# Column tiles of 64 for every matmul but the transposes, with a new order of the period's steps, in a two-layer graph network kernel

## The chip, the cores and the metric

The kernel runs on one core of one Trainium2 chip. The metric is the device time of one execution in microseconds (us). PE is the matrix engine, DVE the vector engine, ACT the scalar engine, POOL the GpSimd engine and SP the engine whose queue issues most DMAs. PSUM is the memory that PE writes, in banks of 2 KB in each of 128 partitions; SBUF is the working memory.

## The reference

There are B = 128 graphs of N = 128 nodes with F = 64 features, in fp32. Layer 0 is an edge network over the nonzero entries of `adj`, layer 1 a three-layer network over aggregated features. Both are residual with a layer norm.

```python
# layer 0: mask of edges, an edge function relu(a_j + c_k) summed over k
mask = (adj > 0)
diff = x[:, :, None, :] - x[:, None, :, :]
h  = relu((x @ W1a)[:, :, None, :] + diff @ W1b + b1)       # H = 192
hm = einsum('bjkh,bjk->bjh', h, mask)
x  = layernorm(x + hm @ W2 + deg[..., None] * b2)
# layer 1
agg = einsum('bmn,bnd->bmd', adj, x)
h = elu(agg @ V1 + c1); h = elu(h @ V2 + c2)                  # 128 wide
out = layernorm(x + h @ V3 + c3)
```

## The kernel before

Two graphs are taken together as one pair p, so that 2 x 64 features fill 128 partitions; there are 64 pairs. Everything in layer 0 is sparse. Nodes are sorted by their degree (`prepare`: the mask `mk`, degrees `deg`, `keys`, ranks, a permutation `permb`), and nine blocks of sorted nodes (`BLOCKS`: first node, last node, slots) give each node as many slots as its degree may need. In `sort_mask` nine instructions `oh` on DVE write, for each block, a one-hot matrix of the neighbour that sits in each slot, by comparing `vp` with `slotc`, both in SBUF, in bf16. For each pair and block there is a unit of three steps: ACT copies `aj` into a PSUM bank `e` (L914), PE adds the gathered `cp[k]` of the neighbours, as 18 matmuls of 64 output partitions (L924), and DVE sums absolute values over the slots (`sums`, L934). `cp` holds the projected features in three bf16 parts that add up to fp32; `project_c` makes it (C, L712 and L715, two banks, then `r` L726 on DVE, `cp` L722 and L729 on ACT and L731 on POOL). `sort_x` sorts the features and projects them to `aj` (L610, L617), and then makes a correction for unused slots: `sa` on POOL (L624), the `short` product, `ea` on DVE (L639) and `corr` on POOL (L646). `turn` transposes `adj` and `x`. `finish` is the rest of the pair: `hm` on POOL (L846), projections (L851, L855), un-sorting (L868), `y` and its statistics `st` on DVE (L741, L746), the factors `ve`, `rs`, `nb` on POOL (L753 to L758; `rs` is a power on 128x2 elements), the normed `x` on ACT (L775), then aggregation (L875), `hid1` (L884), `hid2` (L890) and `last` (L895, L897) with ELU steps `r` and `e` on ACT and `h` on DVE between them, and a second norm that ends in the stored output.

All queues are written out by a planner at build time, the class `Flow`. A thread is a generator of steps; a step names its engines, a planned cost, the events that it follows, and how many of the four shared PSUM banks it takes. Each step has a due time in `DUE`, in us from the start of its pair's period, to which `ROUND` = 11.1651 is added for each pair; a negative time is a step made ahead for a later pair. From the first gather until 14 units before the end the planner takes, among the steps that could be planned, the one with the earliest due time. So in each period the order of an engine's queue is that of the due times modulo 11.1651. A list in `DUE` has one time for each step that a thread yields, in order: the last nine of `sort_mask` are the `oh` of units 0 to 8, the last four of `sort_x` are `sa`, `short`, `ea` and `corr`, the first two of `prepare` are `mk` and `keys`, and the last of `project_c` is its step on POOL; a unit has three, for copy, gather and sum. Before and after that stretch it takes the step that is ready first by its planned clocks. The chip executes each engine's queue in order, and waits only for data and for buffers to come free; the planned times do not hold anything back. Two things in the planner stand for the chip: `PORT` is a resource that POOL's steps and the `oh` steps take in turn, and `CHANGE` is a price for PE going from one tiling of its array to another. The modes are "" (full width of 128 columns), "t" (column tiles, 128 rows by 64 columns), "r" (row tiles, 64 by 128), "x" (transposes), and "*", which is column tiles if the step before it was in them and full width otherwise. `stationary` writes a "*" product in the form that the mode asks for:

```python
if flow.mode == "t":
    for h in (slice(0, P // 2), slice(P // 2, P)):
        nc.tensor.matmul(out[h], lhsT(h), rhs, **kw)
else:
    nc.tensor.matmul(out, lhsT(slice(0, P)), rhs, **kw)
```

The edge banks `e` are four, used in turn by the units, so a unit's copy follows the sum of the unit four before it. The last pair's norms are done partly on DVE (`LATE`). After the sparse part, a dense path exists for pairs whose degrees exceed the slots; it is passed over when a count on the chip says that there are none.

Of the kernel before, what the change touches and what calls it, by code (L numbers as in the profile page):

```python
# [87 lines left out]
class Flow:  # L88
# [61 lines left out]
    def _kind(self, mode):  # L150
        return mode if mode != "*" else "t" if self.mode == "t" else ""
# [35 lines left out]
def sparse(tc, env):  # L187
# [18 lines left out]
        "prepare": (-43.06, -42.93, -39.21, -39.08, -35.87),  # L206
        "sort_x": (-26.76, -10.46, -10.33, -3.14, -3.02, 2.5, 2.63, 2.76, 2.89),
        "sort_mask": (-26.12, -25.99, -25.86, -23.42, -23.29, -23.16, -13.67, -13.28, -13.03,
                      -12.77, -2.63, -2.25, -1.99, -1.73),
        "turn": (-36.9, -36.77),  # L210
        "project_c": (-32.15, -29.32, -29.2, -29.07, -28.94, -4.17, -4.04),
        "finish": (12.64, 19.44, 19.57, 21.62, 21.75, 21.88, 22.01, 28.04, 28.17, 29.2, 33.56,
                   33.69, 33.82, 34.71, 43.31, 43.44, 44.47, 44.6, 46.52, 46.65, 48.06, 48.19,
                   59.87),
        "unit": [(-1.48, 0.96, 1.09), (2.12, 2.25, 2.37), (3.02, 3.14, 3.27), (3.66, 3.79, 3.91),
                 (4.68, 4.81, 4.94), (5.07, 5.2, 5.33), (5.97, 6.1, 6.22), (6.35, 6.48, 6.61),
                 (7.25, 11.61, 11.74)],
    }

    DUE["consts_late"] = (  # L220
        12.0, 17.0, 18.5, 19.5, 19.65, 19.66, 19.67, 19.68, 23.0, 24.0, 25.0, 26.0, 27.0, 28.0,
        29.0, 30.0, 31.0, 32.0, 33.0, 34.0, 35.0, 36.0)
# [23 lines left out]
    def stationary(out, lhsT, rhs, **kw):  # L246

        if flow.mode == "t":
            for h in (slice(0, P // 2), slice(P // 2, P)):
                nc.tensor.matmul(out[h], lhsT(h), rhs, **kw)  # L250
        else:
            nc.tensor.matmul(out, lhsT(slice(0, P)), rhs, **kw)  # L252
# [287 lines left out]
    def prepare(p):  # L540
# [19 lines left out]
        def spread(key):  # L560
            for s in range(2):
                stationary(key[:, s * N:(s + 1) * N],
                           lambda h: degb[:, s:s + 1].to_broadcast([P, h.stop - h.start]),
                           identb, start=True, stop=True)
            stationary(key[:, 2 * N:3 * N], lambda h: small[:, h], iotb, start=True, stop=True)
        ev, key = yield ("PE:*", 0.17, [ev] + made("identb", "small", "iotb"), 1, spread)
# [37 lines left out]
    def project_a(p, xsT, ev):  # L604
# [3 lines left out]
        def project(aps):  # L608
            for c in range(3):
                nc.tensor.matmul(aps[:, c * N:(c + 1) * N], wad[:, c, :], xsT,  # L610
                                 start=True, stop=True)
        ev, aps = yield ("PE", 0.66, [ev] + made("wad"), 1, project)
# [36 lines left out]
    def sort_mask(p, ev):  # L649
# [3 lines left out]
        def sort(t):  # L653
            for s in range(2):
                stationary(t[:, s * N:(s + 1) * N], lambda h: d["mk"][:, s, h], permb[:, s, :],
                           start=True, stop=True)
            for s in range(2):
                stationary(t[:, (2 + s) * N:(3 + s) * N], lambda h: permb[:, s, h], identb,
                           start=True, stop=True)
        ev, t = yield ("PE:*", 0.22, [ev], 1, sort)  # L660
# [7 lines left out]
        ev, vps = yield ("PE:*", 0.12, [evm] + made("prefix"), 1,  # L668
                         lambda vps: stationary(vps[:, :2 * N], lambda h: prefix[:, h], flat(mtp),
                                                start=True, stop=True))  # L670
# [33 lines left out]
    def project_c(p, ev):  # L704

        d = S[p]
        cols = H + O

        def project(*cps):
            for s in range(2):  # L710
                k = slice(s * F, (s + 1) * F)
                nc.tensor.matmul(cps[s][:, :cols], d["turned"][k, 2, :], wc[k, :],  # L712
                                 start=True, stop=False)
            for s in range(2):
                nc.tensor.matmul(cps[s][:, H:cols], onesb[:, :P], b2p, start=False, stop=True)  # L715
        ev, *cps = yield ("PE:r", 0.7, [ev] + made("wc", "b2p", "onesb"), 2, project)
        cp = d["cp"] = prep.tile([P, 3, 2, cols], BF16, name="cp", bufs=7)
        r1 = prep.tile([P, 2, cols], F32, name="r1", bufs=4)
        hi = []
        for s in range(2):  # L720
            e, = yield ("ACT", act(cols), [ev], 0,
                        lambda: nc.scalar.copy(cp[:, 0, s, :], cps[s][:, :cols]))  # L722
            hi.append(e)
        for s in range(2):
            ev, = yield ("DVE", dve(cols), [hi[s]], 0,
                         lambda: nc.vector.tensor_sub(r1[:, s, :], cps[s][:, :cols],  # L726
                                                      cp[:, 0, s, :]))
            flow.give(cps[s], ev)
        ev, = yield ("ACT", act(2 * cols), [ev], 0, lambda: nc.scalar.copy(cp[:, 1], r1))  # L729
        ev, = yield ("POOL PORT", 1.12, [ev], 0,  # L730
                     lambda: nc.gpsimd.tensor_sub(cp[:, 2], r1, cp[:, 1]))  # L731
        happened(ev, "cp", p)
# [106 lines left out]
    def finish(p):  # L839
# [8 lines left out]
        def project(yb):  # L848
            cp, mtp = d["cp"], d["mtp"]
            for c in range(3):  # L850
                nc.tensor.matmul(yb[:, :2 * O], hm[:, c, :], flat(w2d[:, c]),  # L851
                                 start=(c == 0), stop=False)
            for s in range(2):
                for i in range(3):
                    nc.tensor.matmul(yb[:, s * O:(s + 1) * O], mtp[:, s, :], cp[:, i, s, H:H + O],  # L855
                                     start=False, stop=(s == 1 and i == 2))
        ev, yb = yield ("PE", 0.85, [ev] + made("w2d"), 1, project)
# [8 lines left out]
        def unsort(t):  # L866
            for s in range(2):
                nc.tensor.matmul(t[:, s * O:(s + 1) * O], d["permT"][:, s, :],  # L868
                                 ys[:, s * O:(s + 1) * O], start=True, stop=True)
        ev, t = yield ("PE", 0.4, [ev, event("permT", p)], 1, unsort)  # L870
# [11 lines left out]
        def hidden1(zb):  # L882
            for s in range(2):
                nc.tensor.matmul(zb[:, s * N:(s + 1) * N], v1p[:, s, :], agg,  # L884
                                 start=True, stop=True)
        ev, zb = yield ("PE", 0.49, [ev] + made("v1p"), 1, hidden1)
        h1, ev = yield from elu(zb, ev, "h1", 0)

        def hidden2(zb):
            nc.tensor.matmul(zb[:, :2 * N], v2s, h1, start=True, stop=True)  # L890
        ev, zb = yield ("PE", 0.48, [ev], 1, hidden2)
        h2, ev = yield from elu(zb, ev, "h2", 1)

        def last(t):
            nc.tensor.matmul(t[:, :2 * O], onesb[:, :P], c3p, start=True, stop=False)  # L895
            for s in range(2):
                nc.tensor.matmul(t[:, s * O:(s + 1) * O], h2[:, s * N:(s + 1) * N], v3s,  # L897
                                 start=False, stop=(s == 1))
        ev, t = yield ("PE", 0.51, [ev] + made("rowp", "v3s"), 1, last)
# [283 lines left out]
```

## Time and profile before

| | |
|---|---|
| median of 3 runs | 752.73 us (752.58 to 753.43) |
| the profiled execution | 754.12 us |
| its span, first to last instruction | 752.3 us |
| mean granted PE clock | 0.992 |
| period in the steady part | 11.18 us, 64 pairs |
| first `sums` of the first pair's last block | 33.1 us after the start |
| HBM traffic | 23 GB/s over the span |

The profile is of one execution. Its page gives the busy time of each engine (PEld is the loading of weights, beside PE), and the chain of work that ended last. Views of the trace give the busy time of each engine in a stretch (the columns are start and end, length, then PE, PEld, DVE, ACT and POOL, each with its number of instructions, the granted clock, the DMA share and GB/s), and a timeline of instructions in order of time: start, length, engine, line, operation, tiles, shape, number. A length is that of the record, and in the timeline instructions that follow each other in one group are one line; the recorded time of an instruction reaches past the start of the next one, because engines are pipelined. What an instruction costs its engine is therefore read from start to start. On PE, 128*64 is a product over 128 rows into 64 columns of the array; an fp32 product appears as two instructions.

### The profile page before, as it was taken

What the parts mean: (1) busy time and instruction counts of PE and PEld (TensorE: products, weight loads), DVE (VectorE), ACT (ScalarE), POOL (GpSimd) and SP (SyncE); (2) the same over time, 40 slices, a digit from 0 to 9 for tenths busy, and PEclk for the clock granted to TensorE, in tenths of its full rate; (3) what the DMA queues carried; (4) which work ended last, traced back from release to release, by engine and by line L of the source; (5) the groups of instructions that cost most, each with busy time, mean ns of one, the idle gap of its engine ahead of it and who ended that gap; (6) DMA issues with size and microseconds to landing.
All of it is one profiled execution on the core that took longest, in us unless ns stands there. A gap on an engine that the chain in (4) does not pass through costs nothing.

```text
span 752.3 us, 36121 instructions
## 1 busy us (share of the span) xinstructions
PE 732.1 (97%) x14791; PEld 667.8 (89%) x14792; DVE 724.3 (96%) x2381; ACT 706.3 (94%) x1986; POOL 432.1 (57%) x801
## 2 busy tenths in 40 slices
PE   7899999999999999999999999999999999999994
PEld 4788999999999999999999999999999999999993
DVE  7999999999999999999999999999999999999984
ACT  4778999999999999999999999999999999999984
POOL 5336557556556556656655655655755655655662
PEclk9999999999999999999999999999999999999997
DMA  4000011011101101101101101101101110110000
GB/s 124 15 3 3 21 27 31 23 26 31 26 21 31 30 18 31 30 19 31 31 17 31 32 16 33 31 21 27 31 24 25 31 26 22 31 27 10 10 14 19
DMA packets 54667, 19.72 MB, mean 26 GB/s; under 512 B 37600, under 2 KB 54496, under 8 KB 54496
## 3 DMA queue, kind: packets, MB, share of 16 engines
q1 hardware_dynamic: 53792, 17.05, 9.3%
q8 instruction: 118, 1.93, 1.1%
q14 instruction: 53, 0.43, 0.2%
q10 hardware_dynamic: 704, 0.30, 0.1%
HBM read 13.14 MB, written 4.19 MB: 23 GB/s over the span
## 4 chain that ended last, share of the span: by engine, by line
PE 93%; DVE 3%; ACT 2%; issue 1%; DMA 0%; POOL 0%; ACTq 0%; POOLq 0%; DVEq 0%
PE e L924 45%; PE m L610 6%; PE m L851 5%; PE m L712 5%; PE m L890 4%; PE m L884 4%; PE m L897 4%; PE m L868 3%; PE m L694 3%; PE m L250 3%; PE m L596 2%; PE m L875 2%; PE m L855 1%; PE m L715 1%; PE m L252 1%; PE m L695 1%
## 5 line engine op out<-in xcount | busy, mean ns | idle before, releaser
L924 PE MATMUL e<-oh,cp 128*64 128x162 bf16 (+3 forms) x10368 | 385.5, 228 | 3.5 <-ACT e L914 3.3
L924 PEld LDWEIGHTS <-cp 128*64 128x64 bf16 x10368 | 350.2, 110 | 16.6 <-issue 4.9
L934 DVE TENSOR_REDUCE sums<-e 128x54 f32<-128x486 f32 (+8 forms) x576 | 335.1, 611 | 6.8 <-PE e L924 2.0
L914 ACT COPY e<-aj 128x504 f32<-128x504 f32 (+6 forms) x576 | 293.6, 542 | 8.0 <-DVE sums L934 7.4
L753 POOL TENSOR_SCALAR ve<-st 128x2 f32<-128x2 f32 x126 | 24.1, 191 | 242.4 <-DVE st L746 232.0
L679 DVE TENSOR_TENSOR oh<-vp,slotc 128x308 bf16<-128x308 bf16 (+6 forms) x576 | 150.3, 321 | 1.0 <-ACT vp L672 0.2
L754 POOL TENSOR_TENSOR rs<-ve,mhalf 128x2 f32<-128x2 f32 x126 | 87.8, 697 | 10.5
L731 POOL TENSOR_TENSOR cp<-r,cp 128x512 bf16<-128x512 f32 x64 | 74.3, 1160 | 29.8 <-ACT cp L729 29.8
L646 POOL TENSOR_TENSOR corr<-ea,sa 128x384 f32<-128x384 f32 x64 | 64.2, 1003 | 9.9 <-DVE ea L639 4.9
L624 POOL TENSOR_TENSOR sa<-aj,srow 128x384 f32<-128x384 f32 x64 | 64.6, 1009 | 2.9 <-ACT aj L617 2.9
L795 ACT ACTIVATE r<-m,cc 128x256 f32<-128x256 f32 x128 | 61.4, 480 | 5.1 <-PE m L884 3.1
L846 POOL TENSOR_TENSOR hm<-sums,corr 128x384 f32<-128x384 f32 x63 | 63.3, 1004 | 5.1 <-DVE sums L934 5.1
L617 ACT ACTIVATE aj<-m,b1c 128x128 f32<-128x128 f32 x192 | 56.6, 365 | 8.2 <-PE m L610 1.8
L801 DVE SCALAR_TENSOR_TENSOR h<-m,cc,e 128x256 f32<-128x256 f32 x128 | 60.6, 473 | 2.0 <-ACT e L798 1.9
L798 ACT ACTIVATE e<-r 128x256 f32<-128x256 f32 x128 | 54.4, 426 | 2.1
L610 PE MATMUL m<-xsT,wad 128*128 128x128 f32 x384 | 54.4, 278 | 0.0
L851 PE MATMUL m<-w2d,hm 128*128 128x128 f32 x384 | 53.7, 276 | 0.0
L775 ACT ACTIVATE x<-y,nb,rs 128x64 f32<-128x64 f32 x126 | 49.1, 442 | 0.2 <-POOL nb L757 0.2
L610 PEld LDWEIGHTS m<-xsT,wad 128*128 128x128 f32 x384 | 48.5, 194 | 0.3
L726 DVE TENSOR_TENSOR r<-m,cp 128x256 f32<-128x256 f32 x128 | 47.9, 416 | 0.5 <-ACT cp L722 0.5
L851 PEld LDWEIGHTS m<-w2d,hm 128*128 128x128 f32 x384 | 48.0, 192 | 0.4 <-POOL hm L846 0.4
L712 PE MATMUL m<-wc,turned 64*128 64x256 f32 x256 | 46.4, 436 | 1.7 <-DVE r L726 1.7
(157 smaller groups left out, 1333.1 us busy)
## 6 DMA issues: line engine op xcount, KB each, us to landing
adj<-in_adj_dram SPq DMA_DIRECT2D x64, 128.0 KB, 2.7
xx<-in_x_dram SPq DMA_DIRECT2D x64, 64.0 KB, 2.7
out_dram<-o SPq DMA_DIRECT2D x64, 64.0 KB, 1.6
w1s<-in_L_gnn_W_dram ACTq DMA_DIRECT2D x2, 96.0 KB, 3.0
w2s<-in_L_gnn_W_dram ACTq DMA_DIRECT2D x2, 48.0 KB, 2.6
v2s<-in_L_gnn_W_dram SPq DMA_DIRECT2D x1, 64.0 KB, 2.2
v1d<-in_L_gnn_W_dram SPq DMA_DIRECT2D x2, 32.0 KB, 2.2
rows<-in_L_gnn_b_dram SPq DMA_DIRECT2D x1, 64.0 KB, 4.8
```

Of the source, the lines that this page charges most:

```text
L610: nc.tensor.matmul(aps[:, c * N:(c + 1) * N], wad[:, c, :], xsT, start=True, stop=True)
L624: evs, = yield ("POOL PORT", 1.0, [have] + made("srow"), 0, lambda: nc.gpsimd.tensor_mul(sa, aj, srow))
L646: ev, = yield ("POOL PORT", 1.05, [ev, evs], 0, lambda: nc.gpsimd.tensor_sub(corr, ea, sa))
L679: lambda: nc.vector.tensor_tensor(oh[:, 2 * base:2 * (base + n)].rearrange("p (b s w) -> p b s w", b=2, w=w), vp[:, :, p0:p1].rearrange("p ...
L712: nc.tensor.matmul(cps[s][:, :cols], d["turned"][k, 2, :], wc[k, :], start=True, stop=False)
L731: lambda: nc.gpsimd.tensor_sub(cp[:, 2], r1, cp[:, 1]))
L754: nc.gpsimd.tensor_tensor(rs, ve, mhalf, op=OP.pow)
L846: lambda: (nc.vector if late else nc.gpsimd).tensor_sub(hm, d["sums"], d["corr"]))
L851: nc.tensor.matmul(yb[:, :2 * O], hm[:, c, :], flat(w2d[:, c]), start=(c == 0), stop=False)
L914: lambda: nc.scalar.copy(e.rearrange("p (c s w) -> p c s w", c=3, w=w), d["aj"][:, :, p0:p1].rearrange("p c (o w) -> p c o w", o=1) .to_br ...
L924: nc.tensor.matmul(e[s * HB:(s + 1) * HB, c * n:(c + 1) * n], cp[:, k, s, c * HB:(c + 1) * HB], oh[:, 2 * base + s * n:2 * base + (s + 1) ...
L934: nc.vector.tensor_reduce(d["sums"][:, :, p0:p1], e.rearrange("p (c s w) -> p c w s", c=3, w=w), AX.X, OP.add, apply_absolute_value=True)
```

## The change

All products except the transposes are written as column tiles: a product into 128 partitions becomes two of 64, on the two column halves of the array. `stationary` and the mode "*" go, and `tiled` does it for bf16 and fp32 alike. C, which is two row tiles of 64 by 128, becomes four tiles of 64 by 64. The due times of all steps are new, and with them the order of the queues and how many periods a pair is spread over; some planned costs of PE steps are lower. The number of instructions on DVE, ACT and POOL does not change, nor what they compute.

```diff
     def _kind(self, mode):
-        return mode if mode != "*" else "t" if self.mode == "t" else ""
+        return mode
...
     DUE = {
-        "prepare": (-43.06, -42.93, -39.21, -39.08, -35.87),
-        "sort_x": (-26.76, -10.46, -10.33, -3.14, -3.02, 2.5, 2.63, 2.76, 2.89),
-        "sort_mask": (-26.12, -25.99, -25.86, -23.42, -23.29, -23.16, -13.67, -13.28, -13.03,
-                      -12.77, -2.63, -2.25, -1.99, -1.73),
-        "turn": (-36.9, -36.77),
-        "project_c": (-32.15, -29.32, -29.2, -29.07, -28.94, -4.17, -4.04),
-        "finish": (12.64, 19.44, 19.57, 21.62, 21.75, 21.88, 22.01, 28.04, 28.17, 29.2, 33.56,
-                   33.69, 33.82, 34.71, 43.31, 43.44, 44.47, 44.6, 46.52, 46.65, 48.06, 48.19,
-                   59.87),
-        "unit": [(-1.48, 0.96, 1.09), (2.12, 2.25, 2.37), (3.02, 3.14, 3.27), (3.66, 3.79, 3.91),
-                 (4.68, 4.81, 4.94), (5.07, 5.2, 5.33), (5.97, 6.1, 6.22), (6.35, 6.48, 6.61),
-                 (7.25, 11.61, 11.74)],
+        "prepare": (-24.5978, -24.0014, -22.9112, -21.9409, -21.6704),
+        "sort_x": (-20.6913, -15.0087, -14.4632, -12.0858, -11.7997, 1.8348, 1.8461, 2.1939,
+            4.62),
+        "sort_mask": (-18.1457, -17.8686, -17.7351, -15.4178, -14.5485, -11.9667, -10.5327,
+            -5.7425, -3.4278, -3.4268, -1.4564, -0.3543, 3.6441, 5.5231),
+        "turn": (-22.6987, -21.5267),
+        "project_c": (-20.3395, -20.3385, -17.5988, -16.6899, -16.6889, -9.7271, -2.2404),
+        "finish": (14.2885, 17.5657, 18.9157, 21.5273, 21.7549, 22.7104, 25.0457, 25.7472,
+            26.8309, 29.8992, 29.9002, 30.1973, 31.0217, 31.5164, 32.8762, 32.8772, 33.4708,
+            34.6785, 35.5058, 36.3339, 37.111, 38.1205, 40.4445),
+        "unit": [(-1.48, 0.7058, 2.0416), (-0.624, 0.2732, 0.5961), (-0.6296, 0.4835, 3.0319),
+            (-0.0537, 3.6599, 4.551), (3.0229, 4.3955, 6.8908), (1.0857, 3.9125, 7.977), (5.289,
+            7.7684, 9.129), (6.6931, 7.5648, 8.2583), (7.8545, 10.296, 10.5304)],
...
-    def stationary(out, lhsT, rhs, **kw):
...
+    HALVES = (slice(0, P // 2), slice(P // 2, P))
+
+    def tiled(out, lhsT, rhs, **kw):
+
+        for h in HALVES:
+            nc.tensor.matmul(out[h], lhsT[:, h], rhs, **kw)
...
-                nc.tensor.matmul(aps[:, c * N:(c + 1) * N], wad[:, c, :], xsT,
-                                 start=True, stop=True)
-        ev, aps = yield ("PE", 0.66, [ev] + made("wad"), 1, project)
+                tiled(aps[:, c * N:(c + 1) * N], wad[:, c, :], xsT, start=True, stop=True)
+        ev, aps = yield ("PE:t", 0.66, [ev] + made("wad"), 1, project)
...
-                nc.tensor.matmul(cps[s][:, :cols], d["turned"][k, 2, :], wc[k, :],
-                                 start=True, stop=False)
+                for h in HALVES:
+                    nc.tensor.matmul(cps[s][h, :cols], d["turned"][k, 2, h], wc[k, :],
+                                     start=True, stop=False)
...
-        ev, *cps = yield ("PE:r", 0.7, [ev] + made("wc", "b2p", "onesb"), 2, project)
+        ev, *cps = yield ("PE:r PE:t", 0.6, [ev] + made("wc", "b2p", "onesb"), 2, project)
...
-                nc.tensor.matmul(t[:, s * O:(s + 1) * O], d["permT"][:, s, :],
-                                 ys[:, s * O:(s + 1) * O], start=True, stop=True)
-        ev, t = yield ("PE", 0.4, [ev, event("permT", p)], 1, unsort)
+                tiled(t[:, s * O:(s + 1) * O], d["permT"][:, s, :], ys[:, s * O:(s + 1) * O],
+                      start=True, stop=True)
+        ev, t = yield ("PE:t", 0.22, [ev, event("permT", p)], 1, unsort)
```

The products of `prepare` and `sort_mask` that went through `stationary`, and `hm`'s and `cp`'s projections, `hid1`, `hid2` and `last`, change to `tiled` in the same manner (`hid1` 0.49 to 0.43, `hid2` 0.48 to 0.43, `last` 0.51 to 0.3 in planned cost). The due times of the constants of layer 1 (`consts_late`, 22 steps made once) run from 10.17 to 29.51 where they ran from 12 to 36.

## The prediction

> **What bounds the kernel now.** I read the page first (busy shares and the chain that ended last), then busy time by stage, then the timeline of one period on each engine. The page and one stage:
>
> ```profile
> PE 732.1 (97%) x14791; PEld 667.8 (89%) x14792; DVE 724.3 (96%) x2381; ACT 706.3 (94%) x1986; POOL 432.1 (57%) x801
> ...
> PE 93%; DVE 3%; ACT 2%; issue 1%; DMA 0%; POOL 0%; ACTq 0%; POOLq 0%; DVEq 0%
> ```
>
> ```profile
> 100.00:400.00 300.00, 300.00 (x6221) 276.19 (x6220) 296.66 (x966) 294.69 (x833) 179.44 (x324) 1.00 0.11 27
> ...
> 710.00:733.00 23.00, 23.00 (x476) 21.39 (x472) 19.92 (x49) 19.70 (x54) 13.54 (x22) 1.00 0.05 11
> ```
>
> PE (third column) is busy for 300.00 of 300 us, and the chain is PE for 93%. DVE (296.66) and ACT (294.69) look as full, but a recorded duration overlaps its successor's, so I count from start to start. The period is 11.18 us (the mask sort starts at 410.11 and 421.29); 64 of them are 715.5 us of the 752.3 us span, the rest is filling and draining. Taking for each DVE instruction the start-to-start time that it has where nothing is late, DVE has **10.82 us** of work a period: nine sums 4.73, nine `oh` 2.07, two `h` 0.78, two `r` 0.66, rank 0.54, `ea` 0.485, two statistics 0.42, two `y` 0.41, `mk` 0.41, `permb` 0.33. The other 0.36 are waits for PE: `y` L741 starts at 414.23 and its successor 0.31 later, where 0.20 is its cost. ACT has 10.6 in the same way. So PE binds, and a faster PE can give at most 0.36 us a period before DVE binds.
>
> **The change on PE.** Timeline of PE in that period (start, length, then the tiles):
>
> ```profile
> 410.22 0.28 PE L250 MATMUL m<-identb,permb 128*64 128x128 bf16 x4
> 410.43 0.44 PE L694 MATMUL m<-ident,adj 128*128 128x128 f32 x2
> ...
> 412.33 0.68 PE L890 MATMUL m<-h,v2s 128*128 128x256 f32 x2
> 412.85 0.27 PE L252 MATMUL m<-mtp,prefix 128*128 128x256 bf16 x1
> 412.96 0.56 PE L868 MATMUL m<-ys,permT 128*128 128x64 f32 x4
> 413.35 0.66 PE L884 MATMUL m<-agg,v1p 128*128 128x128 f32 x4
> 413.94 0.85 PE L924 MATMUL e<-oh,cp 128*64 128x170 bf16 x18
> 414.63 0.39 PE L596 MATMUL m<-permf,xx 128*64 128x128 f32 x4
> 414.85 0.80 PE L924 MATMUL e<-oh,cp 128*64 128x162 bf16 x18
> ```
>
> An fp32 product is two passes. L596 is fp32 already in two column tiles: 4 instructions in 0.22 us (414.63 to 414.85), 0.11 for a pair of passes of 128 columns. A full-width fp32 pass of 128 columns costs the same 0.11, so L610 and L851 gain nothing (0.67 to 0.65 each). L868 streams only 64 columns, yet takes 0.39/4 = 0.10 a pass: its weight load (mean 191 ns for 128 columns) is the limit. In tiles the loads are 64 wide (137 ns at L596, two started 3 ns apart), so I take 64/128 of 0.11: 0.056 a pair, 0.22 for L868 (−0.17), and L897 likewise 0.45 to 0.22 (−0.22). If those loads did not overlap, both keep their time and PE is 0.4 worse. L890 loses an exposed load (0.52 to 0.43), L884 too (−0.06). Switches: a pair after L250 would have started at 410.33, and the first of three 0.11 transposes leaves the group 0.16 late; from full width to gathers (L884 to L924) costs 0.12, and before that happens twice (also after L897). After, only transposes to tiles pays it: −0.12. C keeps a change in and out (0.10 each) and an exposed load: its tiles run side by side as its two row tiles do now, 0.79 either way; four side by side is not in the trace, and if they ran two by two it is +0.43. Small bf16 steps: L855's 6 full instructions (412.16 to 412.33, 29 ns each) become 6 pairs at about 31 ns, the spacing of the 66-column gather (18 in 0.31): +0.015. A bf16 load takes 98 ns for 128 columns and 110 for 64, each hidden behind streams that are 29 ns or more apart. The Trainium skill (TensorEngine Tiling (Array Packing), "Gotcha 2: Feature Incompatibilities") has a rule against the change here, that column tiling excludes fast weight load; as the rows above hide the load, the sum is the same by the rule and by the rows. In total 0.17+0.22+0.09+0.06+0.12+0.03−0.015 = 0.68 less: PE falls from 11.18 to **10.5** (10.9 to 11.3 with the bad ends).
>
> **The change of order.** Due times modulo 11.1651 give each engine's queue. On DVE: ..., `mk` (8.898), sums of unit 6 (9.129), first `h` (9.186), `oh` of unit 5 (9.709), `oh` of unit 0 (10.363). On POOL: `keys` (9.494), then at once `sa` (1.835 of the next), first factors, `hm`, `corr`, second factors, `cp` (8.925). `oh` reads two SBUF tiles, and this trace shows what a POOL instruction does to it:
>
> ```profile
> 18.02 1.89 DVE L679 TENSOR_TENSOR oh<-vp,slotc 128x224 bf16<-128x224 bf16 x4
> ...
> 18.52 1.27 POOL L731 TENSOR_TENSOR cp<-r,cp 128x512 bf16<-128x512 f32 x1 [0.78 <-ACT cp L729]
> ```
>
> Four `oh` should last 0.9 us; the one that came after POOL's start at 18.52 ended at 19.90, and it alone costs 0.24: it began 0.13 before POOL's end at 19.79. The three other such meetings (`sa` at 21.76, `cp` at 710.89 and 720.62) give 0.13 too. In the steady periods no `oh` meets POOL: all nine lie in POOL's hole.
>
> ```profile
> 410.07 1.16 POOL L731 TENSOR_TENSOR cp<-r,cp 128x512 bf16<-128x512 f32 x1 [0.40 <-ACT cp L729]
> 414.93 0.19 POOL L753 TENSOR_SCALAR ve<-st 128x2 f32<-128x2 f32 x1 [3.70 <-DVE st L746]
> ```
>
> The new order spreads the nine over the period, in six places. Nothing but `keys` holds `sa` back: its `aj` was due 13.6 us earlier. How soon it follows the second `mk`, with POOL idle, is seen where that `mk` starts at 59.52:
>
> ```profile
> 59.94 0.18 POOL L556 CAST degb<-degs 128x2 bf16<-128x2 f32 x1 [0.70 <-DVE mk L549]
> 60.09 0.19 POOL L557 TENSOR_TENSOR keyc<-degs,jcol 128x2 f32<-128x2 f32 x1
> 60.23 1.00 POOL L624 TENSOR_TENSOR sa<-aj,srow 128x384 f32<-128x384 f32 x1
> ```
>
> 0.72 after that start. So `sa` keeps `oh` out until 0.72+1.00−0.13 = 1.59 after it, while DVE gets there after `mk` 0.20, sums 0.60, `h` 0.39 = 1.19. DVE stands 0.40, and everything behind it with it. The other places by the same counting from `st`, `ea` and second `st`, which gate POOL: `oh` of unit 7 arrives 1.495 after `ea` starts and `corr` lets go at 1.495; units 2 and 8 fall between `corr` and `cp` (which starts 0.15 after unit 8's `oh` is done); units 3 and 4 come 0.07 after `cp`; units 6 and 1 are free of large POOL work. Each costs 0, with margins of 0.1. DVE's period: 10.82 + 0.40 = **11.22**, against 11.18.
>
> The other edits: depth between `prepare` and the end of `finish` falls from 103 to 65 us by the due times; the same work is done, so nothing in the steady part. The last 14 units are ordered by readiness in both kernels; from 710 to 733 us PE alone is full (23.00 against 19.92), and 6% less PE work there gives −1.4. The constants' new due times move 22 steps once, under 1 us of either sign. DMAs move with `begin`, over 20 us ahead of use.
>
> **Sum.** +0.04 × 62 periods = +2.8, −1.4: +1.4 on the span of 752.3, whose execution took 754.12; the median is 752.73, so I apply the difference to that: **754.1 us**. With 0.05 either way on the stall and 1.5 on the ends its own range is 747 to 762.
>
> **Rivals.** *Faster: the port meeting is absent.* If `oh` of unit 5 is issued before `sa`, that is if `sa` starts over 1.19 after the second `mk` or POOL runs late, DVE has 10.82 and the next loop decides: PE from the gather of unit 1 to the mask sort (gathers 0.31, 0.65, 0.63, 0.44, 0.60, short 0.11, C 0.79, last 0.28, sort 0.22 = 4.03), 0.29 to ACT, and on ACT from `mtp` to the next copy for unit 1 (0.27+0.26+0.26+0.51+0.52+0.48+0.16+0.16+0.25+0.53+0.16+0.51+0.32+0.50+0.75+0.52+0.40 = 6.56): 10.88. That is −0.30 × 62 − 1.4 = −20: 733 us. Against it: `sa` has no other wait. *Much slower: POOL's short power holds `oh` as well.* `rs` works on 128x2 but lasts 0.70. Second factors: `rs` runs from 1.99 to 2.69 after `ea`'s start and `oh` of unit 2 arrives at 2.14: +0.42; then `cp` gets in ahead of the `oh` of unit 8, as at 18.52: +1.03; first factors: +0.2. 12.87 a period, 752.7 + 1.69 × 62 − 1.4 = 856 us. For it: every POOL tensor instruction that an `oh` met held it. Against: the release comes before POOL's end, so with its reads, and two columns are read early. The skill's SBUF — State Buffer, "Who interferes with whom", has the pair held for the whole instruction; by that alone it would be 856. No `oh` meets `rs` in this trace. *Slower by other waits.* Four banks serve more steps in a row (`hid1` takes the bank of `agg` one thousandth of a unit later; C takes that of `permb`), and margins of 0.1 are missed: +0.2 to +0.6 a period, 765 to 790. *fp32 tiles not side by side*: PE +3 us a period, over 900; L596 excludes it.
>
> **Chances.** The forecast 0.42, faster rival 0.21, other waits 0.20, `rs` 0.16, tiles 0.01. The forecast's own spread around 0.2% (1.5 us, about what can be told from no change) is 0.12 faster, 0.10 same, 0.20 slower. So 0.33, 0.10, 0.57. The range leaves out the 0.17 of the two worst: 731 to 790.
>
> **What would show it.** Right: PE below 96% busy in the stages, no L868 spacing of 0.11; in each period one `oh` (unit 5) of 0.7 us beside `sa`, the other eight short; DVE in the chain. Wrong: `oh` beside `rs` or `cp` lengthened (that rival), all nine short and the period at 10.9 (the faster one), PE or ACT waiting on DVE's bank releases (other waits).

## The result and the profile after

The changed kernel takes **759.33 us** (median of 4 runs, 759.19 to 759.39) against 752.65 us of the kernel before beside it: a ratio of 1.0086, 95% interval 1.0069 to 1.0104. It is slower, as forecast, and inside the range; the forecast of 754.1 named 1.4 us of loss, and 6.7 came, in other places than those named. The profiled execution took 759.34 us with a span of 757.5; that of before had 752.3, so the two traces differ by 5.2 us. (The other 1.4 lie in before: its profiled execution is that much above its median, the changed kernel's is not.)

The page of the changed kernel, busy shares and the chain that ended last, and two of its stages (columns as before: PE is the third, DVE the fifth):

```profile
PE 713.3 (94%) x17375; PEld 633.5 (84%) x17376; DVE 733.8 (97%) x2381; ACT 703.2 (93%) x1986; POOL 432.7 (57%) x801
...
DVE 79%; PE 12%; issue 4%; ACT 3%; DMA 0%; POOL 0%; ACTq 0%; POOLq 0%; DVEq 0%
```

```profile
100.00:400.00 300.00, 291.68 (x7272) 261.18 (x7268) 300.00 (x966) 293.05 (x833) 177.94 (x322) 1.00 0.11 27
710.00:733.00 23.00, 21.04 (x541) 18.85 (x536) 23.00 (x58) 20.77 (x56) 15.05 (x25) 1.00 0.04 10
```

PE and DVE have changed places: DVE is full in both stages, PE is not, and the chain is DVE for 79% where it was PE for 93%. The steady period is 11.18 us, the same as before to 0.01. The cause of that is in the timelines of DVE and POOL in one period:

```profile
405.06 0.47 DVE L798 SCALAR_TENSOR_TENSOR h<-m,cc,e 128x256 f32<-128x256 f32 x1
405.45 0.95 DVE L675 TENSOR_TENSOR oh<-vp,slotc 128x308 bf16<-128x308 bf16 x2
406.33 0.67 DVE L929 TENSOR_REDUCE sums<-e 128x51 f32<-128x510 f32 x1
...
411.96 0.57 DVE L675 TENSOR_TENSOR oh<-vp,slotc 128x336 bf16<-128x336 bf16 x2
412.46 0.40 DVE L723 TENSOR_TENSOR r<-m,cp 128x256 f32<-128x256 f32 x1
```

```profile
404.81 0.20 POOL L555 TENSOR_TENSOR keyc<-degs,jcol 128x2 f32<-128x2 f32 x1
404.96 1.00 POOL L620 TENSOR_TENSOR sa<-aj,srow 128x384 f32<-128x384 f32 x1
...
411.81 0.70 POOL L751 TENSOR_TENSOR rs<-ve,mhalf 128x2 f32<-128x2 f32 x1
412.47 1.16 POOL L728 TENSOR_TENSOR cp<-r,cp 128x512 bf16<-128x512 f32 x1
```

The two `oh` at 405.45 (units 5 and 0) last 0.88 until the sums start at 406.33; apart they cost 0.24 and 0.25. The first of them takes 0.63 from start to start in all the steady periods but two (0.55 and 0.83), 0.39 too much, beside `sa`, which runs from 404.96 to 405.96. The two `oh` at 411.96 take their usual 0.50 although `rs` runs over both. Eight of the nine cost what they do without POOL, to 0.04. On PE:

```profile
400.79 0.39 PE L871 MATMUL m<-turned,x 128*64 128x128 f32 x4
401.14 0.88 PE L250 MATMUL m<-w2d,hm 128*64 128x128 f32 x12
...
405.45 0.40 PE L250 MATMUL m<-ys,permT 128*64 128x64 f32 x8
405.68 0.60 PE L250 MATMUL m<-h,v2s 128*64 128x256 f32 x4
...
409.08 0.66 PE L709 MATMUL m<-wc,turned 64*64 64x256 f32 x8 [0.30 <-ACT e L909]
...
409.82 0.40 PE L250 MATMUL m<-v3s,h 128*64 128x64 f32 x8
```

The un-sorting takes 0.23 (405.45 to 405.68) where it took 0.39, and the fp32 tiles do run side by side. PE now waits, 0.30 of it ahead of C.

Where the 5.2 us of span lie is seen from the start of the last block's `sums` of pairs 4, 59 and 63, in the trace of each kernel:

| | pair 4 | 4 to 59 (55 periods) | 59 to 63 | to the end |
|---|---|---|---|---|
| before | 79.68 | 614.98 | 37.95 | 19.7 |
| changed | 81.92 | 615.20 | 41.18 | 19.2 |
| difference | +2.24 | +0.22 | +3.23 | −0.5 |

So the steady part is even, and the loss is in the filling and the draining. That is a question of its own beside the one that the prediction was mostly about.

### The profile page after: what moved, and what is told of

It is laid out like the page before. It is cut to its first block, busy times and chain, and to the rows that moved or that the text cites. A ratio compares the mean times of both kernels' runs of the same rounds, so it can differ in the third digit from the quotient of the medians.

```text
span 757.5 us, 41220 instructions
## 1 busy us (share of the span) xinstructions
PE 713.3 (94%) x17375; PEld 633.5 (84%) x17376; DVE 733.8 (97%) x2381; ACT 703.2 (93%) x1986; POOL 432.7 (57%) x801
## 4 chain that ended last, share of the span: by engine, by line
DVE 79%; PE 12%; issue 4%; ACT 3%; DMA 0%; POOL 0%; ACTq 0%; POOLq 0%; DVEq 0%
DVE sums L929 32%; DVE oh L675 17%; DVE h L798 6%; PE e L919 5%; DVE r L723 5%; DVE cmp L569 5%; PE m L250 5%; DVE ea L635 3%; DVE y L738 3%; DVE mk L547 3%; DVE st L743 2%; DVE permb L576 2%; ACT e L909 1%; PE m L709 1%; PE m L690 1%
## 5 line engine op out<-in xcount | busy, mean ns | idle before, releaser
L919 PE MATMUL e<-oh,cp 128*64 128x66 bf16 (+3 forms) x10368 | 401.6, 228 | 4.6 <-ACT e L909 3.7
L919 PEld LDWEIGHTS <-cp 128*64 128x64 bf16 x10368 | 359.1, 111 | 16.1 <-issue 15.0
L909 ACT COPY e<-aj 128x504 f32<-128x504 f32 (+6 forms) x576 | 305.9, 552 | 18.1 <-DVE sums L929 17.4
L675 DVE TENSOR_TENSOR oh<-vp,slotc 128x336 bf16<-128x336 bf16 (+6 forms) x576 | 190.3, 356 | 0.0
L751 POOL TENSOR_TENSOR rs<-ve,mhalf 128x2 f32<-128x2 f32 x126 | 87.6, 696 | 10.5
L554 POOL CAST degb<-degs 128x2 bf16<-128x2 f32 x64 | 11.8, 184 | 139.0 <-DVE mk L547 139.0
L709 PE MATMUL m<-wc,turned 64*64 64x256 f32 x512 | 43.2, 403 | 17.6 <-ACT e L909 17.6
L250 PE MATMUL m<-xsT,wad 128*64 128x128 f32 x768 | 55.8, 280 | 1.7 <-DVE r L723 0.9
L250 PE MATMUL m<-w2d,hm 128*64 128x128 f32 x768 | 55.9, 278 | 0.7 <-DVE hm L843 0.6
L719 ACT CAST cp<-m 128x256 bf16<-128x256 f32 x128 | 48.7, 382 | 4.0 <-PE m L250 3.3
L250 PEld LDWEIGHTS m<-w2d,hm 128*64 128x64 f32 x768 | 42.5, 136 | 11.7 <-issue 10.6
```

The costliest lines, as they stand in the source:

```text
L250: nc.tensor.matmul(out[h], lhsT[:, h], rhs, **kw)
L675: lambda: nc.vector.tensor_tensor(oh[:, 2 * base:2 * (base + n)].rearrange("p (b s w) -> p b s w", b=2, w=w), vp[:, :, p0:p1].rearrange("p ...
L751: nc.gpsimd.tensor_tensor(rs, ve, mhalf, op=OP.pow)
L909: lambda: nc.scalar.copy(e.rearrange("p (c s w) -> p c s w", c=3, w=w), d["aj"][:, :, p0:p1].rearrange("p c (o w) -> p c o w", o=1) .to_br ...
L919: nc.tensor.matmul(e[s * HB:(s + 1) * HB, c * n:(c + 1) * n], cp[:, k, s, c * HB:(c + 1) * HB], oh[:, 2 * base + s * n:2 * base + (s + 1) ...
```

## Experiments on the steady period

**oh_before_h**: one due time, so that `oh` of unit 5 stands 0.39 us nearer to `mk`.

```diff
-            -5.7425, -3.4278, -3.4268, -1.4564, -0.3543, 3.6441, 5.5231),
+            -5.7425, -3.4278, -3.4268, -2.0151, -0.3543, 3.6441, 5.5231),
```

> The changed kernel with one due time moved: `oh` of unit 5 goes on DVE between the sums of unit 6 and the first `h`, that is 0.39 us earlier after `mk`, still behind it; the same work, nothing left out. POOL lets go 1.59 us after the second `mk` starts in either place, so DVE waits 0.39 longer. Theory (port meeting): the stall grows from 0.40 to about 0.79, the period to 11.57 and the time to about 783 us (781-786). Rival (PE or ACT sets the period, or the stall is a fixed price of being beside `sa`): no change, 757-761.

788.28 us, ratio 1.0462 (1.0445 to 1.048); period 11.68. DVE in one period:

```profile
408.03 1.10 DVE L674 TENSOR_TENSOR oh<-vp,slotc 128x308 bf16<-128x308 bf16 x1
409.05 0.47 DVE L797 SCALAR_TENSOR_TENSOR h<-m,cc,e 128x256 f32<-128x256 f32 x1
```

This `oh` now takes 1.02 from start to start, 0.78 more than its 0.24, with `sa` running from 407.94 to 408.94. The stall is not a fixed price: it lasts until POOL lets go, wherever DVE arrives. The period rose by 0.49, 0.10 more than the stall did; the chain has PE in it now, as DVE's later `h` feeds PE.

**oh_before_mask**: both `oh` ahead of `mk`.

```diff
-        "sort_mask": (-18.1457, -17.8686, -17.7351, -15.4178, -14.5485, -11.9667, -10.5327,
-            -5.7425, -3.4278, -3.4268, -1.4564, -0.3543, 3.6441, 5.5231),
+        "sort_mask": (-18.1457, -17.8686, -17.7351, -15.4178, -14.5485, -13.48, -10.5327,
+            -5.7425, -3.4278, -3.4268, -2.32, -0.3543, 3.6441, 5.5231),
```

> The changed kernel with two due times moved, so that `oh` of unit 5 and of unit 0 are issued on DVE before the second `mk` instead of after it; the same work, nothing left out. POOL's `sa` starts only after `mk` and `keys`, so no `oh` meets it. Theory (the stall of 0.40 us a period under `sa` sets the period): DVE falls to its 10.78 of work, or the loop over PE and ACT decides at 10.88, so the period goes from 11.18 to 10.8-10.9 and the time from 759 to 738-743 us. Rival (the period of 11.18 is a limit of PE or ACT that the stall only fills): still 757-760. Rival (`oh` moved earlier meets the end of another POOL instruction): a lengthened `oh` elsewhere, and a time between.

757.50 us, ratio 1.0057 (1.0041 to 1.0074); period 11.15. All nine `oh` are short, DVE has 0.37 us of waits in each period, and almost nothing is won: the number of the theory was wrong by 15 us and more. The chain says what has come in the place of the stall (start, length, what):

```profile
404.38 0.40 DVE h L797
404.78 0.04 issue
404.82 0.82 PE m L249 x10
405.64 0.37 PE m L689 x2
406.01 0.11 PE m L690
406.12 1.69 PE e L918 x54
...
407.92 0.59 PE m L708 x8
408.51 0.50 PE m L249 x14
409.01 0.02 issue
409.04 0.29 DVE y L737
```

From the end of the first `h`, PE works through its queue for 4.26 us without a gap, and only at its end is the last layer's product, for which `y` on DVE waits; from `y` DVE needs 6.89 to the end of the next `h`. Together 11.15. The two `oh` lie in the second stretch there; after `h`, they lie beside PE's stretch and cost nothing. Two experiments follow from this.

**obm_pe_more**: the same order, and 0.43 us more of PE in that loop.

```diff
             tiled(zb[:, :2 * N], v2s, h1, start=True, stop=True)
+            tiled(zb[:, :2 * N], v2s, h1, start=True, stop=True)
```

> The run with both `oh` ahead of `mk`, and on PE the product of the second hidden layer (`v2s` by `h`) made twice into the same bank, which leaves the result as it is: 4 more instructions, 0.43 us of PE a period, in the stretch between the first `h` and `y`. Theory (in that order the loop of PE from `h` to `y` and DVE from `y` to `h` sets the period, not PE's sum): the period goes up by the whole 0.43, 11.15 to 11.58, and the time from 757.5 to 783 us, although PE had waits of some 0.2 us a period. Rival (DVE alone is the limit, its waits being short ones of its own): under 765 us.

786.84 us, ratio 1.0449 (1.0432 to 1.0467); the period is 11.58 to 11.60. The loop it is.

**sums8_first**: both `oh` on the far side of the sums of unit 8.

```diff
-        "sort_mask": (-18.1457, -17.8686, -17.7351, -15.4178, -14.5485, -11.9667, -10.5327,
-            -5.7425, -3.4278, -3.4268, -1.4564, -0.3543, 3.6441, 5.5231),
+        "sort_mask": (-18.1457, -17.8686, -17.7351, -15.4178, -14.5485, -11.7802, -10.5327,
+            -5.7425, -3.4278, -3.4268, -0.6251, -0.3543, 3.6441, 5.5231),
```

> The changed kernel with two due times moved the other way: `oh` of unit 5 and of unit 0 are issued on DVE behind the sums of unit 8 instead of before them; the same work, nothing left out. They then reach DVE 0.20+0.60+0.39+0.59 = 1.78 us after the second `mk` starts, and POOL lets go 1.59 after it: no meeting. And, unlike in the run with both `oh` ahead of `mk`, they stay out of the stretch from `y` to the first `h` on DVE. Theory (two limits: the stall, and a loop first `h` - PE's queue up to the last layer - `y` - DVE's steps up to `h`, which took 4.26+6.89 = 11.15 with the two `oh` inside and has 0.49 less without them, 10.66): the period falls to DVE's work, 10.78 to 10.85, and the time by 0.33 to 0.40 x 60 periods, to 735-740 us. Rival (the 11.15 of that run is a limit of PE, ACT or the banks that this order has wherever `oh` stands): 11.1 a period, 754-758.

749.90 us, ratio 0.9957 (0.9943 to 0.9971): with two due times moved the new order beats the kernel before. The period is 11.02, under the rival's 11.1 but not the 10.8 of the theory. Its chain, and DVE behind `mk`:

```profile
ACT 62%; PE 24%; DVE 7%; issue 5%; DMA 1%; ACTq 0%; POOL 0%; POOLq 0%; DVEq 0%
```

```profile
401.20 0.47 DVE L798 SCALAR_TENSOR_TENSOR h<-m,cc,e 128x256 f32<-128x256 f32 x1
401.81 0.69 DVE L929 TENSOR_REDUCE sums<-e 128x51 f32<-128x510 f32 x1
402.41 0.57 DVE L675 TENSOR_TENSOR oh<-vp,slotc 128x308 bf16<-128x308 bf16 x2
```

The two `oh` are short (0.49 for both), so the stall is gone. But DVE stands 0.22 between `h` and the sums of unit 8 (0.61 from start to start where `h` costs 0.39), and a chain of ACT and PE sets the period: a third limit, 0.16 below the stall's period. Which of its waits is the decisive one I did not separate.

**pe_more**: the extra product of obm_pe_more, in the changed kernel as it is.

> The changed kernel with the product of the second hidden layer made twice on PE, into the same bank, which leaves the result as it is: +0.43 us of PE a period. Theory (DVE with its stall sets the period; the loop from `h` over PE to `y` and back has 10.66 and would have 11.09): no change in the steady period, 11.18, and a time of 759 to 762 us. Rival (PE, 97% busy in the stages, still sets it): +0.43 in each of 62 periods, 786.

764.11 us, ratio 1.0140 (1.0125 to 1.0156). The steady period is 11.20, that is +0.01 for 0.43 us more PE: PE did not bind the changed kernel. It is 2 us above what I allowed, in the drain and the tail (+1.2 and +2.6). The stage says how close it was:

```profile
100.00:400.00 300.00, 299.92 (x7373) 266.58 (x7371) 300.00 (x966) 292.93 (x832) 177.73 (x322) 1.00 0.11 27
```

PE is full again at 11.20, and the chain is PE for 89%. So PE's own work in the changed kernel is 11.20 − 0.43 = 10.77 us a period.

## Experiments on the two halves of the change

**tiles_old_order** has the changed kernel's products with the due times of the kernel before, **full_new_order** the reverse.

```diff
-        "prepare": (-24.5978, -24.0014, -22.9112, -21.9409, -21.6704),
+        "prepare": (-43.06, -42.93, -39.21, -39.08, -35.87),
...
```

> The tiling of the change alone: every matmul but the transposes in column tiles, with the order of the kernel before; the same work. In that order all nine `oh` lie in POOL's hole, so no stall. Theory (PE's part of the change is worth 0.6 to 0.7 us a period and DVE binds next at 10.82, or the PE and ACT loop at 10.88): period 10.8-10.95, and fill and drain as before: 728-738 us. If the old order makes DVE wait for PE as it did before (0.36 a period, 0.1 of it kept): up to 748. Rival (tiles give PE nothing): 752.

> The order of the change alone: the kernel before, matmuls at full width as they were, with the changed kernel's due times; the same work. The same meeting of `oh` and `sa` is in it (DVE at least 11.18 a period), and PE changes more often between full width and column tiles than before, 5 excursions instead of 3 at 0.10 to 0.16 each way, on top of its 11.18. Theory (the order costs by itself, the tiles gain by themselves): PE 11.5 to 11.9 a period, and fill and drain as in the changed kernel: 775 to 805 us. Rival (the order costs only through the stall): 757 to 762.

| | old order | new order |
|---|---|---|
| full-width products | 752.7, period 11.18 | 820.92, ratio 1.0900 (1.0882 to 1.0918), period 12.13 |
| column tiles | 740.37, ratio 0.9830 (0.9814 to 0.9847), period 10.99 | 759.33, period 11.18 |

The tiles alone win 1.7%; the order alone costs 9%. The stages of the two, tiles in the old order first:

```profile
100.00:400.00 300.00, 295.80 (x7404) 267.33 (x7400) 298.48 (x984) 294.10 (x848) 181.99 (x332) 1.00 0.11 27
```

```profile
100.00:400.00 300.00, 300.00 (x5646) 257.38 (x5640) 280.89 (x890) 272.76 (x768) 165.52 (x299) 1.00 0.10 25
```

In the second PE is full and DVE is not, and the stall is absent in all but two of the periods (`oh` comes as `sa` ends): PE alone takes 12.13 for the products that take 11.18 in the old order, 0.95 more. Most of the groups that grew stand beside a change of mode: the first projection 0.87 from start to start (0.67), the gathers 5.58 (5.33), the last transpose 0.20 (0.11), the `short` product 0.15 (0.06). The aggregation (0.35, from 0.22) grows as much in the changed kernel, where its mode does not change. I had allowed 11.5 to 11.9. So the new order needs the tiles, worth 12.13 − 10.77 = 1.36 in it.

**tiles_old_h**: the 740.37 us version with the first `h` moved ahead of one block of sums.

```diff
-                   33.69, 33.82, 34.71, 43.31, 43.44, 44.47, 44.6, 46.52, 46.65, 48.06, 48.19,
+                   33.69, 33.82, 34.1, 43.31, 43.44, 44.47, 44.6, 46.52, 46.65, 48.06, 48.19,
```

> The run with the tiles alone in the order of the kernel before (10.99 a period, 740 us), and one due time more moved: the first `h` of a pair (due 34.71, now 34.1) goes on DVE ahead of one block of sums instead of behind it, 0.55 us earlier; the same work, nothing left out. In that run DVE waits 0.44 and 0.10 us for PE ahead of and in the rank, and PE waits 0.15 us a period with a small product that needs a bank which this `h` reads last. Theory (that loop, `h` - PE - rank - DVE up to `h`, sets the 10.99, and DVE's work of 10.82 comes next): 10.82 to 10.9 a period, 730 to 737 us, the shortest of all. Rival (the 10.99 is set by another bank or by ACT): 739 to 741; and slower if the sums that `h` now precedes hold up the next gathers.

740.39 us, ratio 0.9831 (0.9818 to 0.9845), period 10.99: nothing. The chain went over another way (PE, then `aj` and `vp` on ACT, `oh`, `y` and `h` on DVE) at the same length. The waits that the expectation put ahead of and in the rank are not there: from start to start the sums ahead of the rank take 0.55 and its two steps 0.27 each, as in the changed kernel. By the same counting DVE has 10.78 of work in both runs and loses 0.21 in two other places, 0.10 where the last `oh` comes late, for `vp` on ACT, and 0.11 here (tiles_old_order):

```profile
407.50 0.28 DVE L739 TENSOR_TENSOR y<-m,xx 128x128 f32<-128x128 f32 x1
407.82 0.30 DVE L744 BATCH_NORM_STATS2 st<-y 128x6 f32<-128x128 f32 x1
```

`st` reads the `y` just ahead of it and starts 0.31 after it, behind its recorded end; in the changed kernel an `oh` stands between the two and follows `y` after 0.20. So DVE has no other wait in the 10.99; what the period would be without these two stays open. The tiles in the old order are the best kernel of this study.

## Experiments on the ends

**prep_earlier**: the preparation one period earlier, in the same order within the period.

```diff
+    for name, n in (("prepare", 5), ("sort_x", 5), ("sort_mask", 12), ("turn", 2),
+                    ("project_c", 7)):
+        DUE[name] = tuple(t - ROUND if i < n else t for i, t in enumerate(DUE[name]))
```

> The changed kernel with every step of the preparation (prepare, turn, the projections of C, the first five sort_x and the first twelve sort_mask) due one period (11.165) earlier: the same order within a period, and one more pair in hand when the last-block sums start; nothing left out. Theory (the 5 us of the changed kernel's loss that the steady periods do not hold come from a shallower pipeline: DVE idles in the fill and has that preparation still to do in the drain): the steady period stays 11.18, and up to one period's preparation moves from the drain into the idle fill: 2 to 5 us less, 754 to 757. Rival (the ends lose for another reason, such as the order of the last units): 758.5 to 760.

760.46 us, ratio 1.0101 (1.0084 to 1.0118): no gain. The drain from pair 59 to 63 did shorten, from 41.18 to 37.85, to what it is before (37.95), but pair 4 came at 87.26 instead of 81.92 (this fill has its dip of the clock too, to 0.50 from 24 to 30 us), and from pair 63 to the end it takes 20.8 instead of 19.2. Against what was expected the steady period fell as well, to 11.12: `sa` starts 0.56 ahead of this `oh` instead of 0.49, which then stands 0.32 beside it instead of 0.39, and the 55 periods are 3.4 us shorter. Depth moves work from the drain to the fill, and the fill was not idle for lack of work. The theory was half right and of no use.

**old_fill3**: the due times of before (`FIRST`) for the first three pairs.

```diff
...
-        flow.start(ROUND * p, DUE[name], gen)
+        flow.start(ROUND * p, (FIRST if p < 3 else DUE)[name], gen)
...
-        flow.start(ROUND * p, DUE["unit"][i], lane(u, ev))
+        flow.start(ROUND * p, (FIRST if p < 3 else DUE)["unit"][i], lane(u, ev))
```

> The changed kernel with the due times of the kernel before for pairs 0, 1 and 2 alone, and its own from pair 3 on; nothing left out. The steady period keeps its stall, 11.18. Theory (the ends lose because in the new order DVE does 5.9 us less work between 10 and 30 us, being the tail of a chain of short steps there, and DVE then does it in the drain): fill of the kernel before, so the last sums of pair 4 at about 79 us instead of 81.9, and up to 5 us less in all: 753 to 757. Rival (the drain loses by its own order): the fill's 2 to 3 us come back at most, and less if the change-over from one order to the other costs something: 757 to 760.

762.67 us, ratio 1.0131 (1.0114 to 1.0148). Pair 0 came 3.8 us earlier (29.45), but pair 4 only 0.4 (81.51), and pair 5 later (93.99 for 93.04): the change-over took back what was won. For the theory this settles nothing.

What I had missed is in the column of the granted clock. The fill of the changed kernel in stretches of 2 us (PE third, clock third from the end):

```profile
16.00:18.00 2.00, 1.18 (x28) 0.90 (x24) 1.26 (x6) 1.96 (x7) 0.79 (x1) 1.00 0.77 194
18.00:20.00 2.00, 1.07 (x14) 0.46 (x14) 0.70 (x3) 1.52 (x6) 2.00 (x3) 1.00 0.00 0
20.00:22.00 2.00, 1.30 (x12) 1.04 (x13) 1.20 (x5) 0.70 (x3) 0.37 (x1) 0.62 0.00 0
22.00:24.00 2.00, 0.81 (x24) 0.81 (x25) 0.00 (x0) 1.51 (x5) 0.00 (x0) 0.50 0.00 0
24.00:26.00 2.00, 2.00 (x34) 2.00 (x31) 0.52 (x2) 1.14 (x2) 0.38 (x1) 0.50 0.00 0
```

PE is busy a little over half the time from 14 to 20, and then gets half its clock until about 27, just when the first gathers run. A second dip follows: PE is idle for 1.86 us, from 52.02 to 53.88, and its clock is 0.50 from 54.6 to 58.

**fill_busy** keeps PE busy there, with 34 calls of this in the gaps (7 after the `vp` product of pair 0, 6 after its `short`, 7 after C and 14 after the projection to `aj` of pair 1):

```diff
+            tiled(edges[3][:, :2 * P], identb, onesb, start=False, stop=True,
+                  skip_group_check=True)
```

> The changed kernel with 34 extra pairs of bf16 matmuls of 256 columns put on PE between 14 and 23 us, in the gaps in which it waits in the fill, into a bank that no unit uses yet; every other instruction keeps its place, nothing left out. Theory (the fill is late because PE, busy for 1.07 to 1.18 us in each 2 us from 14 to 20, is granted a clock of 0.50 to 0.67 from 20.5 to 27 us, so that the first gathers take 3.18 instead of 1.77 us, C 1.27 instead of 0.78 and a projection 1.31 instead of 0.90): the clock stays at 1.0 in the fill, the last-block sums of pair 4 come 2 to 2.4 us earlier, near 79.6 instead of 81.92, and the time falls by as much, to about 757 us; the steady period and the drain stay. Rival (the fill is late by its chain of steps, whatever the clock): pair 4 within 0.5 us of 81.9 and the time 759 to 760.

757.62 us, ratio 1.0064 (1.0051 to 1.0078). The same stretches, and the first gathers in the changed kernel and here:

```profile
18.00:20.00 2.00, 1.87 (x30) 1.07 (x28) 0.70 (x4) 1.53 (x6) 2.00 (x3) 1.00 0.04 6
20.00:22.00 2.00, 1.93 (x36) 1.93 (x38) 1.08 (x5) 1.12 (x5) 0.26 (x1) 1.00 0.00 0
22.00:24.00 2.00, 1.81 (x58) 1.64 (x54) 0.52 (x2) 1.34 (x4) 0.00 (x0) 1.00 0.03 8
```

```profile
23.19 3.18 PE L919 MATMUL e<-oh,cp 128*64 128x66 bf16 x54 [1.71 <-ACT e L909]
```

```profile
22.66 1.76 PE L928 MATMUL e<-oh,cp 128*64 128x66 bf16 x54 [0.19 <-ACT e L918]
```

The clock stays at 1.00, the gathers take 1.76 instead of 3.18, the second dip is gone too, and pair 4 comes at 79.69, 2.23 us earlier (pair 0 by 1.90) and within 0.01 of the trace of before, whose fill has a dip of its own. The tiles in the old order, with no dip, have pair 4 at 78.58, so 1.11 of fill stays with the new order. The steady part (615.22) and the drain (41.16) have not moved. More work on PE made the kernel 1.7 us shorter (the intervals of the two ratios overlap a little, but the longest execution here, 758.79, is below the shortest of the changed kernel, 759.19; the spans, 757.5 and 755.6, say the same).

## Why the prediction had the sign right, by luck, and the size too small

The sign is luck. The forecast took its loss from the steady periods (+2.8) and a gain from the ends (−1.4). Measured in the two traces, the steady periods lose 0.2 and the ends 5.0: with the ends as forecast, the kernel would have been about 1 us faster. Two sums were off as well: 0.04 × 62 is 2.5, not 2.8, and 0.05 a period with 1.5 on the ends gives 749.5 to 758.7, not 747 to 762.

- **What binds, and the port meeting: right.** DVE stands 0.39 us a period beside `sa`, where 0.40 was worked out, in the one place that was named, and this is what kept the period at 11.18. The Trainium skill (SBUF — State Buffer, "Who interferes with whom") says that a DVE instruction with two SBUF inputs contends with a GpSimd instruction that reads SBUF, and, in its line on DVE's two-port modes, that whoever issues first gets the shared pair for the whole instruction. The first holds in both runs that show the stall. The second, taken over to `oh`, does not quite: 405.45 plus the stall of 0.39 is 405.84, and `sa` ends at 405.96, so `oh` gets in 0.12 ahead of POOL's recorded end.
- **The `rs` rival: refuted.** `oh` beside `rs`, a power on 128x2, has its usual length in every period (0.50 for the two at 411.96). By the same page the two would contend; here the measurement decides.
- **DVE's period: 11.22 was forecast, 11.18 measured.** The work without the stall is 10.79 instead of 10.82 (0.46 for `ea`, where 0.485 was counted). So the steady term was not +2.8 but +0.2. One reading was wrong: the 0.31 from `y` to its successor in the kernel before is no wait for PE. The successor is `st`, which reads that `y`, and it is 0.31 in tiles_old_order and tiles_old_h as well. So of the 0.36 put down to PE, 0.11 was still there when PE got faster.
- **PE: 10.5 was forecast, 10.77 measured** (by pe_more). Un-sorting, the last layer, `hid2` and C came out at the forecast, to 0.02, or below it; the two large projections are 0.03 and 0.04 above it. The largest miss is a group that had no term, the aggregation (L871 above), in column tiles before and after: it takes 0.35 to the start of its successor, where it took 0.22 ahead of gathers (419.81 to 420.03). It is 0.35 in full_new_order too and 0.22 in tiles_old_order, so it belongs to the new order; why is not shown. The term for switches was near: the last step from `last` to the gathers falls from 0.205 to 0.055, that from `hid1` only to 0.103, and coming back from the transposes costs 0.09 (the last transpose 0.203 instead of 0.109, read in pe_more). Going to the transposes costs 0.10 in both kernels and only changed its place (the product ahead of them takes 0.157 instead of 0.055, and the one that was ahead of them 0.112 instead of 0.213), and so did entering C (0.10, now in `short`). The skill (TensorEngine Tiling (Array Packing), "Key Properties") says that a change of mode drains the engine and gives no price; these rows do. The sum was not touched, as PE did not bind, but 10.77 beside DVE's 10.79 left no room at all.
- **The faster rival** was right that the stall could be avoided and wrong on what comes next: its loop had 10.88, but without the stall I measured 11.15 and 11.02 in this order. A list of engine sums does not show such loops; they lay hidden under the stall. The waits of the third rival (0.2 to 0.6 a period) are there as soon as the stall is away.
- **The ends: the step that failed.** The forecast for the ends was −1.4, for less PE work in the drain, and "nothing" for the order's smaller depth. The −1.4 is fair for the tiles alone: in tiles_old_order the drain from pair 59 to 63 is 1.77 shorter than before (36.18). But the new order adds to both ends. In the fill it leaves PE so thinly used that its clock halves, +2.24 (shown by fill_busy). In the drain, with DVE full from 710 to 733 us, it takes 3.23 us more than before, and the cause of that is only in part known. One period more of depth shortens the drain by 3.33 and lengthens what follows by 1.6 (prep_earlier), so depth has a part in it, and what it saves is paid in the fill. In this drain `oh` also stands beside `sa` and `cp` on POOL, by 0.76 at 715.69, 0.72 at 725.71 and 0.81 at 726.66, where the drain of before has 0.25 and 0.13; the forecast counted such meetings in the steady periods alone. No run separates them from depth, and prep_earlier has about as many. "The same work is done" was true, and was no answer to when it is done.
- **The base.** I applied the difference of spans to the median. That was sound, but the profile of before is 1.4 above its median, and has a dip of the clock in its own fill (0.80, 0.50 and 0.84 from 16 to 22 us); the changed kernel has dips in all its runs, to judge by the mean clock (0.989 to 0.992, where fill_busy has 0.994 to 0.997).

## What to carry to other kernels

When a stall or an engine is to be relieved, look for the next loop through several engines (a result, the in-order queue in front of its use, the way back) before the gain is counted from the next engine's sum: here 0.39 us of stall hid limits 0.03 and 0.16 below it. Before a gap is put down to another engine, see whether an instruction reads the result of the one just ahead of it: such a pair cost 0.11 in each period here. Try the parts of a change apart: the tiles were worth 12 us, and the order that came with them took 19 back. And price an order at its ends too, from the granted clock and DVE's busy time in stretches of 2 us.

## What the runs showed of the hardware that I had not expected

PE's clock halves without any long pause. From 14 to 20 us it was busy for 1.17, 1.18 and 1.07 us of each 2, with no gap over 0.9 us, and from 20.5 it got 0.50. The Trainium skill (TensorE: Matmul & The Clock Gate, "Why this matters for your kernels") advises against gaps over 3 us; here the clock fell after gaps of a third of that, with PE busy for 53 to 59% of the time. Busy for 1.87 and 1.93 of 2 it kept the clock, and so it did at 1.25 and 1.59 in the fill of tiles_old_order, between stretches of 1.63 and 1.86. But a low share does not settle it. In full_new_order the clock stays at 1.00 here, although PE is idle for 1.86 us at a stretch, from 31.16 to 33.02:

```profile
30.00:32.00 2.00, 1.16 (x33) 0.96 (x28) 2.00 (x4) 0.00 (x0) 0.64 (x1) 1.00 0.04 8
32.00:34.00 2.00, 0.98 (x10) 0.86 (x12) 2.00 (x6) 1.37 (x4) 0.00 (x0) 1.00 0.02 4
34.00:36.00 2.00, 1.07 (x38) 0.94 (x38) 1.64 (x5) 2.00 (x6) 0.32 (x1) 1.00 0.00 0
```

A pause of the same 1.86 us in the changed kernel, from 52.02 to 53.88, was followed by the half clock. So neither the share nor the gap alone tells when the clock halves, and these runs do not show the rule.
